# Starting the scans of a hybrid attention–MLP–Mamba kernel from 256 tokens of two batches

## The chip, the cores and the metric

The kernel runs on one core of a Trainium2 chip. The metric is the device time of one execution in microseconds. Before the change the median of three runs is 893.15 us (889.9 to 897.59). Engine names are those of the profile: PE is the matrix engine (PEld its weight loads), DVE the vector engine, ACT the scalar engine, POOL the GpSimd engine, SP the engine that issues most DMAs.

## The reference

The input `x` has 4 batches of 1024 tokens with 128 channels. Four residual blocks follow each other:

```
x = x + attention(layernorm(x))          # 16 heads; window of 32 plus every 64th token
x = x + ffn(layernorm(x))                # [h,-h] @ +-1 weights, relu*2, @ +-1, relu*2, @ +-1
x = x + mamba_block(layernorm(x))        # see below; it has its own layernorm and residual
x = x + ffn(layernorm(x))                # the same weights again

mamba_block(x):                          # per batch, E = 256 inner channels, N = 16 states
  xn = layernorm(x) * ln_g + ln_b
  u, z = split(xn @ W_in)
  u2 = silu(causal_conv(u, 4 taps) + conv_b)
  dt_lo, Bm, Cm = split(u2 @ W_xp);  dt = softplus(dt_lo @ W_dt + b_dt)
  h_t = exp(dt_t * A) * h_(t-1) + (dt_t * u_t) * B_t        # sequential over the 1024 tokens
  y_t = sum over N of h_t * C_t;  y = (y + u2 * D) * silu(z)
  return x + res_scale * (y @ W_out)
```

Only the recurrence over `h` ties the tokens of a batch together in order; two batches are independent of each other.

## The kernel before

**Layout.** `x` stays in SBUF as two tiles, one for each pair of batches (`xs[bp]`). A tile of `xs` holds 64 tokens of each batch of the pair, so a chunk `c` of four such tiles is 512 rows: 256 tokens of both batches. A pair has four chunks.

**Stages.** Attention runs first (to about 246 us). Then chunk by chunk: the first MLP (`mlp`, called by `early`), the norms of the Mamba block (`mamba_norm`: statistics, a power on POOL, scaling on ACT, four transposes on PE, and `mxnT`, the transposed rows that the block reads), its preparation (`mamba_pre_half`: convolution folded into eight matmuls `pc`, silu to `u2`, projection `px`, `pd`, softplus to `dt`, the product `du`), then the scans, the output projection (`mamba_out`, `mamba_out_own`) and the second MLP (`late`, `late_batch`).

**Scans.** The scans are cut into eight parts of 512 tokens of one batch, in the order of line 911: for each pair the first halves of both batches, then the second halves. A part has 16 units, one for each state `n`, each over 256 channels (two halves `h` of 128 partitions). One unit is: two decays `da` on ACT into PSUM, one product `db` on POOL, two scans `hs` on DVE (`tensor_tensor_scan`), and the product `hc` with C, on DVE from `pcc` that PE spreads into PSUM, or for three units in sixteen on POOL. Pairs of `hc` are added by a DMA, and PE sums them into `pys`. In a first half a scan starts from 0.0 and its last column is copied into `carry[b % 2]` (one tile per batch, line 904); in a second half it starts from that column.

**Order of work.** MLP, norm and preparation are written as generators that yield a `Piece` with an estimated cost per engine; a `Work` runs one. Ahead of the scans (lines 1390 to 1413, eight PSUM banks) the loop goes round robin over `mamba_norm` of chunks 0 and 1, the preparation of part 0 and two `lanes` of MLP chunks, holding the lanes back only when the preparation's next piece is for PE. Lane 0 starts with chunk 0, lane 1 with chunk 1, then chunks 2 and 3. Inside the scans (from line 1414, three spare banks) `pieces` is called twice in a unit and issues pieces into the gaps by a model of the engines' times and by allowances per unit (`RATES`: 2.9 us of PE, 1.2 of DVE, 2.4 of ACT, 1.2 of POOL). Emission order is kept as program order there. A unit asks ahead for what it needs: `load_b` three units ahead, `drive` two ahead; if the part that they ask for isn't prepared, `ready` (line 1360) issues pieces without regard to allowances until it is. `hurry` (line 991) lifts the allowance of a preparation's PE pieces eight units before its part begins.

Part 0 needs the preparation of 512 tokens of batch 0, and so chunks 0 and 1 through MLP and norm.

Of the kernel before, what the change touches and what calls it, by code (L numbers as in the profile page):

```python
# [26 lines left out]
P = 128  # L27
# [16 lines left out]
def hybrid_kernel(ctx: ExitStack, tc: tile.TileContext, x, Wq, Wk, Wv, Wo, ln_g, ln_b, W_in, conv_w,  # L44
# [789 lines left out]

    def early(bp, c, *args):
        stats = yield from awaited(("a", bp, c))
        tiles = xs[bp][:, 4 * c : 4 * c + 4, :]
        yield from mlp(f"a{bp}_{c}", tiles, True, *args, hasty=bp == 1 and c < HALF, stats=stats)
        fed.add(("a", bp, c))
# [64 lines left out]
    carry = [mw.tile([P, NH, N], F32, name=f"carry{b2}") for b2 in range(2)]  # L904
# [6 lines left out]
    parts_in_order = [(b, f) for bp in range(NP) for f in range(2) for b in (2 * bp, 2 * bp + 1)]  # L911
# [6 lines left out]
    def mamba_norm(bp, c):  # L918
# [5 lines left out]
        before = order_of[2 * bp, f] - 4  # L924
# [4 lines left out]
        yield Piece(gp=2.7)  # L929

        rs = small.tile([P, 5, 4], F32, tag="rs2", name=f"rs_z{u}", bufs=2)
        gp.tensor_scalar_add(rs[:, 0], mv[:, :, 1], EPS)
        gp.tensor_scalar(rs[:, 1], mv[:, :, 1], 1.0 + EPS, EPS * EPS, ALU.mult, ALU.add)
        both = rs[:, 0:2].rearrange("p a n -> p (a n)")
        gp.tensor_tensor(both, both, minus_half, ALU.pow)
        gp.tensor_scalar_mul(rs[:, 4], mv[:, :, 0], -1.0)
        gp.tensor_mul(rs[:, 2:4], rs[:, 0:2], rs[:, 4:5].to_broadcast([P, 2, 4]))
        gp.tensor_scalar_add(rs[:, 0], rs[:, 0], 1.0)
# [15 lines left out]
        yield Piece(sc=1.6, same=True)  # L954
        ln_apply(tiles, tiles, rs[:, 0], rs[:, 2])
        yield evict(sc=0.6)
# [4 lines left out]
        )  # L961
        fed.add(("n", bp, c))

    def gate_of(v, gate, xnT):
        yield fill(1.8, 2, loose=True)
        pz = [bank(f"pz{v}_{h}") for h in range(NH)]
        for h in range(NH):
            te.matmul(pz[h], w_in[:, E + h * P : E + (h + 1) * P], xnT[:, DC - 1 :], start=True, stop=True)
# [4 lines left out]
    def mamba_pre_half(b, f):  # L973

        bp, b2, place = b // 2, b % 2, order_of[b, f]
        yield Piece(
            ready=lambda: all(("n", bp, c) in fed for c in range(f * HALF, (f + 1) * HALF))
# [4 lines left out]
        xnT = mamba_in[bp, f][:, b2, :]  # L982
        gate = m2.tile([P, NH, CH], F32, name=f"gate{v}", tag="gate", bufs=4)
        if place:
            yield from gate_of(v, gate, xnT)
# [12 lines left out]
        for h in range(NH):  # L998
            for k in range(DC):
# [3 lines left out]
                elif k % 2 == 0:  # L1003
                    yield Piece(pe=1.8, urgent=hurry)
                te.matmul(
                    pc[h], w_conv[:, k, h * P : (h + 1) * P], xnT[:, k : k + CH], start=k == 0, stop=k == DC - 1
                )
        yield evict(lump=True, sc=3.9)
# [18 lines left out]
        if not place:  # L1027
            yield Piece(1, evict=True, ve=1.4)
            ve.tensor_copy(bc, px[: 6 * N])
            ve.tensor_sub(res[: 4 * N], px[: 4 * N], bc[: 4 * N])  # L1030
            yield Piece(-1, urgent=hurry, sc=1.8)
        else:
            yield Piece(1, evict=True, sc=1.8)
            sc.copy(bc, px[: 6 * N])
        sc.copy(dtl[6 * N :], px[6 * N : 6 * N + DR])
        sc.copy(w, px[: 2 * N])
        nc.sync.dma_start(bd, w)
        prepared.add((b, f, "b"))
        if not place:
            sc.copy(bc[: 4 * N], res[: 4 * N])  # L1040
        else:
# [11 lines left out]
        yield evict(lump=True, sc=3.9)  # L1053
        for h in range(NH):
            sc.activation(dt[:, h], pd[h], AF.Softplus, bias=bdt_t[:, h : h + 1])
        if not place:
            ve.tensor_sub(res[: 2 * N], res[: 2 * N], bc[: 2 * N])
        yield urgent(sc=0 if place else 0.6)
        if not place:
            sc.copy(bc[: 2 * N], res[: 2 * N])  # L1060
        for h in range(NH):
            yield urgent(gp=1.3)
            gp.tensor_mul(du[:, h], dt[:, h], u2[:, h])
            prepared.add((b, f, h))
        if not place:
            yield from gate_of(v, gate, xnT)

    def mamba_out(bp, f):

        pair = [(2 * bp + b2, f) for b2 in range(2)]  # L1070
        yield Piece(ready=lambda: all(("g", *k) in fed for k in pair), same=True)
        for q in range(HALF):
            yield fill(2.0)
            po = bank(f"pmo{bp}_{f}{q}")
            for b2 in range(2):
                if b2:
                    yield more(2.0)
                gate = mamba_pre[pair[b2]][0]
                for i in range(4):
                    t0 = (4 * q + i) * R  # L1080
# [399 lines left out]
```

## Time and profile before

| | us |
|---|---|
| median of the runs | 893.15 |
| the profiled execution | 896.53 |
| its span, first to last instruction | 894.7 |
| attention ends, first MLP begins | about 246 |
| first scan starts | 322.93 |
| scans, eight parts of 16 units | 322.9 to 852.2 |
| tail after the scans | 852.2 to 894.7 |

| engine | busy us | share of the span |
|---|---|---|
| PE | 757.9 | 85% |
| DVE | 726.9 | 81% |
| POOL | 682.5 | 76% |
| ACT | 606.3 | 68% |

The shares are averages over attention, a lead-in, the scans and a tail, which have different limits; what matters below is the busy time within a stretch. In the lists, a line of a group gives its engine, operation, tiles, shapes and count, then busy time and the mean of one in ns, then the idle time before it and what ended that. The parts of the scans start at 322.9, 388.5, 457.0, 519.7, 588.6, 655.1, 726.8 and 790.2 us.

### The profile page before, as it was taken

To read this page: it belongs to the slowest core of one execution; us is meant where nothing else is said; L and a number is where in the kernel's file an instruction comes from. 1 tells how busy PE (TensorE), PEld (TensorE's weight loads), DVE (VectorE), ACT (ScalarE), POOL (GpSimd) and SP (SyncE) were. 2 spreads that over 40 slices of the span, in tenths; PEclk is the share of its full clock that TensorE was granted. 3 is DMA by queue.
4 is the path that set the end of the run, shared out by engine and by line. 5 is a ranking of instruction groups with operands and counts; after the bars stand their busy time and mean duration, and the time that the engine had idled before them with its cause. 6 is when DMAs were issued, how large, how long until landed. Compare 5 with 4: busy or idle time off the path is not lost. (4 is left out here: it accounts for less than half of the span.)

```text
span 894.7 us, 16435 instructions
## 1 busy us (share of the span) xinstructions
PE 757.9 (85%) x6204; PEld 465.8 (52%) x6204; DVE 726.9 (81%) x970; ACT 606.3 (68%) x1358; POOL 682.5 (76%) x525
## 2 busy tenths in 40 slices
PE   5798878966788977788989788989889689889898
PEld 2455546645667653334546554535545345656567
DVE  6699998999563258898899998898988779999942
ACT  3776656754364488887878778878967766664523
POOL 6689966999342079999989998979979879877800
PEclk9899989997679989797999999899989799999999
DMA  4743133330010036564564656555565545666410
GB/s 127 129 74 73 27 57 68 74 70 2 3 48 1 1 109 155 127 159 129 137 148 130 153 130 153 145 121 138 155 154 133 141 112 150 164 145 153 108 25 19
DMA packets 59808, 92.77 MB, mean 104 GB/s; under 512 B 6200, under 2 KB 39776, under 8 KB 59728
## 3 DMA queue, kind: packets, MB, share of 16 engines
q1 hardware_dynamic: 49488, 58.15, 22.6%
q0 software_dynamic: 9680, 33.30, 19.8%
q8 instruction: 49, 0.80, 0.4%
q10 hardware_dynamic: 560, 0.26, 0.1%
q14 instruction: 31, 0.25, 0.1%
HBM read 52.11 MB, written 4.72 MB: 64 GB/s over the span
## 5 line engine op out<-in xcount | busy, mean ns | idle before, releaser
L57 POOL TENSOR_TENSOR db<-du,bs 128x1024 f32<-128x1024 f32 x128 | 315.6, 2504 | 23.8 <-DVE hs L57 20.1
L57 ACT ACTIVATE da<-dt,a_t 128x512 f32<-128x512 f32 x256 | 175.2, 687 | 107.1 <-DVE hs L57 106.8
L57 DVE TENSOR_TENSOR_SCAN hs<-da,db 128x512 f32<-128x512 f32 x128 | 149.9, 1209 | 29.7 <-ACT da L57 29.5
L57 DVE TENSOR_TENSOR_SCAN hs<-da,carry,db 128x512 f32<-128x512 f32 x128 | 156.7, 1266 | 5.5 <-ACT da L57 5.2
L57 PE MATMUL pys<-hc,ident 128*128 128x512 f32 x258 | 145.3, 649 | 1.9 <-DMA hc<-hc 1.8
L57 DVE TENSOR_TENSOR hc<-hs,pcc 128x1024 f32<-128x1024 f32 x104 | 126.7, 1218 | 22.1 <-PE pcc L57 15.9
L57 POOL TENSOR_TENSOR prodv<-vS,E 128x128 f32<-128x128 f32 (+14 forms) x30 | 69.6, 2319 | 12.2 <-ACT E L57 11.9
L57 PE MATMUL pga<-h1a,w 128*128 128x512 f32 x256 | 72.4, 435 | 5.1 <-ACT u L57 2.9
L57 PEld LDWEIGHTS pys<-hc,ident 128*128 128x128 f32 x258 | 49.6, 208 | 43.6 <-issue 37.2
L57 POOL TENSOR_TENSOR prod<-kv,qs 128x128 f32<-128x128 f32 (+14 forms) x30 | 71.3, 2376 | 1.0 <-DVE or L57 1.0
L57 POOL TENSOR_TENSOR hc<-hs,cs 128x1024 f32<-128x1024 f32 x24 | 58.1, 2421 | 13.6 <-DVE hs L57 11.6
L57 PE MATMUL pc<-mxnT,w_conv 128*128 128x512 f32 x128 | 63.3, 624 | 4.3 <-DVE h1b L57 2.4
L57 PEld LDWEIGHTS pga<-h1a,w 128*128 128x128 f32 x256 | 51.2, 201 | 27.4 <-issue 4.3
L57 POOL DMA_DIRECT2D hc<-hc x63 | 62.7, 995 | 1.8 <-issue 0.9
L57 ACT ACT_TABLE_LOAD x48 | 61.6, 1283 | 3.5 <-issue 2.6
L57 PE MATMUL pcc<-bc,spread 96*128 96x512 bf16 x104 | 42.0, 404 | 22.5 <-DVE hc L57 21.7
L57 ACT ACTIVATE E<-S 128x512 f32<-128x512 f32 (+15 forms) x62 | 26.5, 472 | 38.8 <-DVE S L57 38.6
L57 PE MATMUL ps<-kx,qT 64*32 64x256 f32 x1008 | 46.2, 432 | 6.3 <-DVE S L57 5.0
L57 POOL TENSOR_TENSOR du<-dt,u 128x512 f32<-128x512 f32 x16 | 24.8, 1551 | 29.7 <-ACT dt L57 29.6
L57 PEld LDWEIGHTS pc<-mxnT,w_conv 128*128 128x128 f32 x128 | 25.2, 199 | 37.4 <-issue 31.9
L57 ACT COPY ep<-pt 128x512 f32<-128x512 f32 x32 | 18.8, 587 | 36.4 <-DVE eo L57 36.1
L57 PE MATMUL pgb<-h1b,w 128*128 128x512 f32 x128 | 38.0, 447 | 1.4 <-ACT u L57 1.4
(245 smaller groups left out, 1682.9 us busy)
## 6 DMA issues: line engine op xcount, KB each, us to landing
bs<-bd SPq DMA_DIRECT2D x64, 512.0 KB
hc<-hc POOLq DMA_DIRECT2D x63, 512.0 KB, 4.6
vr<-vd SPq DMA_DIRECT2D x32, 256.0 KB
cs<-bd SPq DMA_DIRECT2D x24, 256.0 KB
vd<-kv SPq DMA_DIRECT2D x8, 256.0 KB
x<-in_L_attn_a_x_dram SPq DMA_DIRECT2D x15, 128.0 KB
kx<-kT SPq DMA_DIRECT2D x104, 16.0 KB
out_dram<-x SPq DMA_DIRECT2D x8, 128.0 KB
```

The source lines that it names most:

```text
L57: ins = getattr(self.engine, name)(*args, **kwargs)
```

## The change

The first two parts are no longer (batch 0, first half) and (batch 1, first half) but two quarters: 256 tokens of both batches side by side, in tiles of the same width of 512. So part 0 needs chunk 0 alone. A quarter's scan of 512 columns becomes two of 256, one per batch, and the second quarter's scans start from `carry`, which is now one tile. `mamba_out` runs per quarter.

Chunk 0's MLP is halved: each lane takes 256 of its 512 rows (`early_half`). The lanes' chunks are then 1, 3, 5, 7 and 2, 4, 6. Ahead of the scans only the two half chunks run at first; then the chain of norm, transposes and preparation of part 0 is issued in its order, and the lanes' next pieces are let in where the model of the engines' times says that they end before the chain's next piece. Chunks 1 to 3 otherwise run among the scans.

Small edits ahead of the first scan: five operations of the first `rs` move from POOL to DVE (the power stays), `mxnT` is written before the scaling of `x`, the split of B and C into three bf16 rows moves behind `pd` and partly from ACT to POOL, `du` of part 0 and half of the first `db` go to DVE.

```diff
         yield Piece(ready=lambda: key in known, same=True)
         return known[key]
 
+    def early_half(lane, *args):
+        stats = yield from awaited(("a", 0, 0))
+        at = slice(2 * lane, 2 * lane + 2)
+        yield from mlp(f"a0_0{lane}", xs[0][:, at, :], True, *args, stats=stats[:, :, at])
+        fed.add(("half", lane))
+        if all(("half", k) in fed for k in range(2)):
+            fed.add(("a", 0, 0))
+
     def early(bp, c, *args):
         stats = yield from awaited(("a", bp, c))
         tiles = xs[bp][:, 4 * c : 4 * c + 4, :]
-        yield from mlp(f"a{bp}_{c}", tiles, True, *args, hasty=bp == 1 and c < HALF, stats=stats)
+        yield from mlp(f"a{bp}_{c}", tiles, True, *args, hasty=c == 1 or (bp == 1 and c < HALF), stats=stats)
         fed.add(("a", bp, c))
...
-    carry = [mw.tile([P, NH, N], F32, name=f"carry{b2}") for b2 in range(2)]
+    carry = mw.tile([P, NH, 2, N], F32, name="carry")
...
-    parts_in_order = [(b, f) for bp in range(NP) for f in range(2) for b in (2 * bp, 2 * bp + 1)]
+    QUARTER = "quarter"
+    QT = CH // 2
+    parts_in_order = [(QUARTER, 0), (QUARTER, 1)]
+    parts_in_order += [(b, f) for bp in range(NP) for f in range(2) for b in (2 * bp, 2 * bp + 1)][2:]
...
         mv = yield from ln_sums(tiles, f"z{u}", soon=bp == 0)
-        yield Piece(gp=2.7)
+        by = ve if bp + c == 0 else gp
+        yield Piece(gp=2.9 if by is ve else 2.7)
 
         rs = small.tile([P, 5, 4], F32, tag="rs2", name=f"rs_z{u}", bufs=2)
-        gp.tensor_scalar_add(rs[:, 0], mv[:, :, 1], EPS)
-        gp.tensor_scalar(rs[:, 1], mv[:, :, 1], 1.0 + EPS, EPS * EPS, ALU.mult, ALU.add)
+        by.tensor_scalar_add(rs[:, 0], mv[:, :, 1], EPS)
+        by.tensor_scalar(rs[:, 1], mv[:, :, 1], 1.0 + EPS, EPS * EPS, ALU.mult, ALU.add)
...
-        yield Piece(sc=1.6, same=True)
-        ln_apply(tiles, tiles, rs[:, 0], rs[:, 2])
-        yield evict(sc=0.6)
+        yield evict(sc=0.75)
         t0 = DC - 1 + c % HALF * 4 * R
         sc.activation(
             mamba_in[bp, f][:, :, t0 : t0 + 4 * R].rearrange("p b (m r) -> p m b r", r=R),
             tp.rearrange("p (m b r) -> p m b r", b=2, r=R), AF.Identity, bias=b_t, scale=g_t,
         )
+        fed.add(("t", bp, c))
+        yield Piece(sc=1.6, same=True)
+        ln_apply(tiles, tiles, rs[:, 0], rs[:, 2])
         fed.add(("n", bp, c))
 
...
+    def tokens_of(b, f):
+
+        if b == QUARTER:
+            return lambda k: mamba_in[0, 0][:, :, f * QT + k : f * QT + k + QT]
+        return lambda k: mamba_in[b // 2, f][:, b % 2, k : k + CH]
+
+    def like_tokens(b, bk):
+        return bk.rearrange("p (b t) -> p b t", b=2) if b == QUARTER else bk
...
+        place = order_of[b, f]
+        needs = [("t", 0, f)] if b == QUARTER else [("t", b // 2, c) for c in range(f * HALF, (f + 1) * HALF)]
         yield Piece(
-            ready=lambda: all(("n", bp, c) in fed for c in range(f * HALF, (f + 1) * HALF))
+            ready=lambda: all(k in fed for k in needs)
             and (place < 4 or ("o", *parts_in_order[place - 4]) in fed),
...
-                    pc[h], w_conv[:, k, h * P : (h + 1) * P], xnT[:, k : k + CH], start=k == 0, stop=k == DC - 1
-                )
-        yield evict(lump=True, sc=3.9)
+                    like_tokens(b, pc[h]), w_conv[:, k, h * P : (h + 1) * P], xnT(k), start=k == 0, stop=k == DC - 1
+                )
+        yield evict(lump=True, sc=3.9 if place else 1.0)
...
-        if not place:
-            yield Piece(1, evict=True, ve=1.4)
-            ve.tensor_copy(bc, px[: 6 * N])
-            ve.tensor_sub(res[: 4 * N], px[: 4 * N], bc[: 4 * N])
-            yield Piece(-1, urgent=hurry, sc=1.8)
-        else:
+        if place:
             yield Piece(1, evict=True, sc=1.8)
             sc.copy(bc, px[: 6 * N])
+        else:
+            yield Piece(1, evict=True, sc=0.6)
         sc.copy(dtl[6 * N :], px[6 * N : 6 * N + DR])
-        sc.copy(w, px[: 2 * N])
-        nc.sync.dma_start(bd, w)
-        prepared.add((b, f, "b"))
-        if not place:
-            sc.copy(bc[: 4 * N], res[: 4 * N])
-        else:
+        if place:
+            sc.copy(w, px[: 2 * N])
+            nc.sync.dma_start(bd, w)
+            prepared.add((b, f, "b"))
             for rows in (4 * N, 2 * N):
...
-        yield evict(lump=True, sc=3.9)
+        if not place:
+            yield Piece()
+            sc.copy(w, px[: 2 * N])
+            nc.sync.dma_start(bd, w)
+            prepared.add((b, f, "b"))
+            ve.tensor_copy(bc, px[: 6 * N])
+            ve.tensor_sub(res[: 4 * N], px[: 4 * N], bc[: 4 * N])
+            gp.tensor_copy(bc[: 4 * N], res[: 4 * N])
+            ve.tensor_sub(res[: 2 * N], res[: 2 * N], bc[: 2 * N])
+            gp.tensor_copy(bc[: 2 * N], res[: 2 * N])
+        yield evict(lump=True, sc=3.9 if place else 1.9)
         for h in range(NH):
             sc.activation(dt[:, h], pd[h], AF.Softplus, bias=bdt_t[:, h : h + 1])
-        if not place:
-            ve.tensor_sub(res[: 2 * N], res[: 2 * N], bc[: 2 * N])
-        yield urgent(sc=0 if place else 0.6)
-        if not place:
-            sc.copy(bc[: 2 * N], res[: 2 * N])
         for h in range(NH):
-            yield urgent(gp=1.3)
-            gp.tensor_mul(du[:, h], dt[:, h], u2[:, h])
+            yield urgent(gp=1.3) if place else urgent(ve=0.6)
+            (gp if place else ve).tensor_mul(du[:, h], dt[:, h], u2[:, h])
             prepared.add((b, f, h))
         if not place:
-            yield from gate_of(v, gate, xnT)
...
+    def mamba_out(bp, f, *quarters):
+
+        pair = [(QUARTER, q) for q in quarters] or [(2 * bp + b2, f) for b2 in range(2)]
...
-                gp.tensor_tensor(dbs[i], mamba_pre[b, f][3], bs.unsqueeze(1).to_broadcast([P, NH, CH]), ALU.mult)
+                if i:
+                    gp.tensor_tensor(dbs[i], mamba_pre[b, f][3], bs.unsqueeze(1).to_broadcast([P, NH, CH]), ALU.mult)
+                    return
+                for h, by in enumerate((ve, gp)):
+                    by.tensor_mul(dbs[i][:, h], mamba_pre[b, f][3][:, h], bs)
...
-                first = carry[b % 2][:, h, n : n + 1] if f else 0.0
-                ve.tensor_tensor_scan(hs[:, h], das.pop((i, h)), db[:, h], first, ALU.mult, ALU.add)
-                done["hs", i, h] = spend("ve", 1.235 if f else 1.175, *after(("da", i, h), ("db", i)))
+                da = das.pop((i, h))
+                spans = [(b2, slice(b2 * QT, (b2 + 1) * QT)) for b2 in range(2)] if b == QUARTER else [(b, slice(0, CH))]
+                for b2, ts in spans:
+                    first = carry[:, h, b2 % 2, n : n + 1] if f else 0.0
+                    ve.tensor_tensor_scan(hs[:, h, ts], da[:, ts], db[:, h, ts], first, ALU.mult, ALU.add)
+                us = (1.235 if f else 1.175) + 0.07 * (len(spans) - 1)
+                done["hs", i, h] = spend("ve", us, *after(("da", i, h), ("db", i)))
...
-            if f == 0:
-                sc.copy(carry[b % 2][:, :, n : n + 1], hs[:, :, CH - 1 :])
+            if b == QUARTER:
+                sc.copy(carry[:, :, :, n], hs.rearrange("p h (b t) -> p h b t", b=2)[:, :, :, QT - 1])
+            elif f == 0:
+                sc.copy(carry[:, :, b % 2, n : n + 1], hs[:, :, CH - 1 :])
             decay(i + 1, 1)
-            done["da", i + 1, 1] = spend("sc", 0.67 if f else 0.86, *after(("hs", i, 1)))
...
-        return [m2.tile([P, 2, CH], F32R, name=f"h1{u}_{f}", tag="hc", bufs=6) for f in range(4)]
...
+
     lanes = [
         Work(stream(
-            early(0, lane, f1, lane, *[in_scan_buffers] * lane),
-            early(0, 2 + lane, f1, lane),
-            early(1, lane, f1, lane),
-            early(1, 2 + lane, f1, lane),
+            early_half(lane, f1, lane, *[in_scan_buffers] * lane),
+            *(early(bp, c, f1, lane) for bp, c in (((0, 1), (0, 3), (1, 1), (1, 3)), ((0, 2), (1, 0), (1, 2)))[lane]),
...
-        first = [
-            Work(stream(*(mamba_norm(0, c) for c in first_half))),
-            Work(mamba_pre_half(*parts_in_order[0])),
-        ]
+        lead, pre = Work(mamba_norm(0, 0)), Work(mamba_pre_half(*parts_in_order[0]))
         turn = 0
-        while (*parts_in_order[0], NH - 1) not in prepared:
+        while ("a", 0, 0) not in fed:
             turn += 1
             if turn == 12:
...
-            wanted = first[-1].may() and "pe" in first[-1].next.us
-            for w in first + ([] if wanted else lanes):
+            for w in lanes:
                 if w.may():
                     w.run()
-        for w in lanes:
-            while w.next.evict or w.held:
-                w.run()
+        aside = True
+        while (*parts_in_order[0], NH - 1) not in prepared:
+            w = lead if ("t", 0, 0) not in fed else pre
+            if not w.count:
+                w.since = lead.since
+            issue(w)
+            if pre.held and lead.next:
+                issue(lead)
+            if aside and (QUARTER, 0, "b") in prepared:
+                aside = False
+                for v in lanes:
+                    while v.next.evict or v.held:
+                        issue(v)
+            for v in lanes:
+                while aside and v.may() and max(ends(v)[0].values(), default=0.0) < w.since + 0.3:
+                    issue(v)
     with banks(SPARE), tc.tile_pool(name="wide", bufs=1, space=PSUM) as wide:
         keep.append(True)
         works.extend([
-            first[-1],
+            pre,
             Work(stream(*(mamba_pre_half(*k) for k in parts_in_order[1:]))),
-            Work(stream(*(mamba_norm(0, c) for c in second_half), *(mamba_norm(1, c) for c in range(CT)))),
-            Work(stream(mamba_out(0, 0), mamba_out(0, 1), *(mamba_out_own(*k) for k in parts_in_order[4:-1]))),
...
-                        ("b", 0, c), [("o", b, c // HALF) for b in range(2)],
+                        ("b", 0, c), [("o", b, c // HALF) for b in range(2)] if c >= HALF else [("o", QUARTER, c)],
```

## The prediction, made before the result was known

> **What bounds the kernel now.** I first cut the execution into stretches and read each engine's busy time in them (from:to, length, then PE, PEld, DVE, ACT, POOL busy with counts, granted PE clock, DMA share, GB/s).
>
> ```profile
> 250.00:281.70 31.70, 30.32 (x153) 25.17 (x152) 12.53 (x24) 13.19 (x27) 8.40 (x13) 0.87 0.07 13
> 281.70:322.90 41.20, 37.85 (x151) 25.67 (x151) 10.36 (x23) 25.93 (x49) 10.70 (x16) 0.96 0.10 34
> 322.90:852.20 529.30, 458.76 (x1642) 257.21 (x1641) 474.26 (x465) 405.47 (x861) 466.39 (x339) 0.92 0.56 140
> 852.20:894.70 42.50, 36.77 (x268) 31.25 (x266) 12.14 (x34) 12.67 (x37) 1.26 (x2) 0.98 0.05 13
> ```
>
> Ahead of the scans PE is busy nearly all the time and DVE two fifths of it or less; in the scans DVE (90%), POOL (88%) and PE (87%) are all near full and none is full. So an early start of the scans helps only if work that leaves the lead-in fits into 55 us of idle DVE and 70 us of idle PE. The parts of the scans show how tight that is:
>
> ```profile
> 322.90:388.50 65.60, 51.66 (x130) 23.75 (x129) 55.99 (x63) 57.92 (x121) 61.40 (x49) 0.82 0.48 128
> 388.50:457.00 68.50, 57.74 (x172) 29.46 (x171) 59.96 (x60) 55.70 (x126) 61.69 (x44) 0.90 0.59 148
> 457.00:519.70 62.70, 56.89 (x241) 35.70 (x240) 60.47 (x57) 51.30 (x123) 57.48 (x49) 0.95 0.52 132
> 790.20:852.20 62.00, 54.20 (x237) 34.49 (x236) 61.32 (x68) 32.50 (x58) 47.59 (x29) 0.95 0.58 140
> ```
>
> The part at 457.0 has PE 91% and DVE 96% busy and is among the shortest; the last is at 99% of DVE. A full PE doesn't by itself slow a part; DVE is the floor. The first two parts, which the change rebuilds, have 9.6 and 8.5 us of idle DVE and 14 and 11 of idle PE, at a lower clock.
>
> The floor of a unit is two scans and, in 13 of 16, one `hc`, from the list of groups:
>
> ```profile
> L57 DVE TENSOR_TENSOR_SCAN hs<-da,db 128x512 f32<-128x512 f32 x128 | 149.9, 1209 | 29.7 <-ACT da L57 29.5
> L57 DVE TENSOR_TENSOR_SCAN hs<-da,carry,db 128x512 f32<-128x512 f32 x128 | 156.7, 1266 | 5.5 <-ACT da L57 5.2
> ```
>
> Two are issued back to back in 2.34 us, `hc` in 1.22: 16 x 2.34 + 13 x 1.22 = 53 us a part, of 62 to 72.
>
> **Part by part. (A) The lead-in.** Four lines of the timeline (start, duration) mark today's chain:
>
> ```profile
> 280.90 0.75 DVE L57 SCALAR_TENSOR_TENSOR x<-pfoa,total,x 128x512 f32<-128x512 f32 x1
> 300.98 7.03 PE L57 MATMUL pc<-mxnT,w_conv 128*128 128x512 f32 x16
> 316.81 1.27 ACT L57 ACTIVATE dt<-pd,bdt 128x512 f32<-128x512 f32 x2
> 322.93 2.34 DVE L57 TENSOR_TENSOR_SCAN hs<-da,db 128x512 f32<-128x512 f32 x2 [8.35 <-ACT da L57]
> ```
>
> Chunks 0 and 1 end their MLP at 281.65; 41.3 us later the first scan starts. In between PE interleaves chunks 2 and 3 with the chain: `pc` waits for 32 `pfoa` (297.4 to 301.1) though `mxnT` is there at 297.0.
>
> *A1, the MLP.* The tail of this kernel runs exactly two halves of 256 rows:
>
> ```profile
> 877.87 2.13 PE L57 MATMUL pfc<-fxnTc,w 128*128 128x256 f32 x16 [0.33 <-ACT fxnTc L57]
> 879.84 7.73 PE L57 MATMUL pgc<-h1c,w 128*128 128x256 f32 x64
> 887.41 3.73 PE L57 MATMUL pfoc<-w,h2c 128*128 128x128 f32 x32
> ```
>
> From the first `pfc` to the last result (891.66) that is 13.8 us. Today chunks 0 and 1 resume at 254.3, when DVE is through the folding of the convolution weights and gives the low halves of `fxnT`, and end at 281.65. After: 254.3 + 13.8 = 268, a half to one us more for the low clock at 250 to 258. T0 = 269, or 264 if the smaller `fxnT` is split before those weights.
>
> *A2, from T0 to the first scan,* with today's rows and nothing in between: statistics of four tiles 1.6; `rs` 2.4 (the power 1.68 stays on POOL, five small operations of about 0.15); `mxn` 1.65; last transpose 0.35; `mxnT` 0.8; `pc` 7.05; second `u` 0.75; second half of `px` 1.0; `dtl` 0.65; sum 16.25. Then ACT copies `w` 0.58, loads a table 1.28, softplus 1.27, a table 1.28, `da` 0.69: 5.1. Beside that `w` goes through DRAM to `bs`: 1.7 us to the issue of `bs` (313.38 to 315.02), which has landed by 320.2, so 5.2 more at most; with half a `db` on DVE that is up to 8.1 after `dtl`. Together 21.4 to 24.4; I take 23. First scan at 292, bounds 286 to 295.
>
> *A3, the clock.* Today chunks 2 and 3 keep PE busy through this chain and the clock reads 1.00 from 300 to 323. After, PE has little for 6 to 7 us before `pc`: the model's rule lets in, by my count of its pieces, the transposes and `pf` of chunk 1 and the transposes of chunk 2, 4 us. Where PE idled today the clock fell (0.69 in 322.9 to 334, `pz` 1.06 instead of 0.45 us). A cold `pc`, `px`, `pd` costs 0 to 9 us; I take 1. [...]
>
> Lead-in: 322.9 to 293, **-30 us** (-21 to -37).
>
> **(B) Halved scans.** No 256-wide scan is in the trace. The nearest pair is the same DVE operation at both widths:
>
> ```profile
> L57 DVE SCALAR_TENSOR_TENSOR h1c<-pfc,h1c 128x256 fp32r<-128x256 f32 x16 | 5.8, 417 | 3.6 <-ACT h1c L57 3.6
> L57 DVE SCALAR_TENSOR_TENSOR h1c<-pfc,h1c 128x512 fp32r<-128x512 f32 x8 | 5.1, 673 | 0.0
> ```
>
> Two halves cost 2 x 417 - 673 = 161 ns more; issued back to back (0.75 for two of 256, 1.29 for two of 512) 0.105 us more. 32 units x 2 = 64 extra scans: 6.7 to 10.3 us. The second quarter starts from `carry` where today's second part starts from 0: 64 scans x 0.047-0.057 = 3 to 3.6. It lies on the engine that is the floor, so I count it in full: **+11** (0 if it only fills idle DVE, at most 14). [...]
>
> **(C) Work that moves in among the scans.** PE: today all of chunks 2 and 3 but 32 `pfoa` is done ahead. After, by my count, chunk 1 lacks 32 `pg` and 32 `pfo` (11.2), chunks 2 and 3 some 13 and 14: 38 less today's 4, so 34 us of PE for 70 idle. DVE: three `x` and 12 `h1` and `fxnT`, less today's one `x` and what is done ahead, about 6, and chunk 1's statistics 1.8: 8 us for 55 idle. In exchange chunks of the second pair (22 us of PE in the second part: 6.9 `pfa`, 10.7 `pga`, 4.0 `pfoa`) move to later parts. If all of it fits: 0. If it displaces PE one for one: +34. The part at 457.0 (91% and 96%) is nearest to what is asked, and it was short: I take **+4**.
>
> **(D) New due times.** The second part's `b` must be ready at unit 13 and its `du` at unit 14, 57 us after the start at 4.1 us a unit. It needs chunk 1. Rest of its MLP: 11.2 us of PE among scans; the nearest row, chunk 3's last 32 `pfoa`, took until 336.4, 13.5 us after the first scan, so 20 to 25. Norm and preparation took 41 us unhindered in the lead-in, and 48 among scans (326.5 to 374.3). So the scans wait 20 + 41 - 57 = 4 us to 25 + 48 - 57 = 16 us. Pieces issued by `ready` don't ask for allowances, so I take the lower end, **+4**. While they wait, PE and ACT work and DVE, POOL stand.
>
> The rest is small: `mamba_out` has as many matmuls as before; `carry` is copied in 32 units as before (185 ns); DMA counts and bytes, SP's queue included, stay; moving `du` and half a `db` to DVE shortens A2 and is in it.
>
> **The sum:** -30 + 11 + 4 + 4 = **-11** us against this execution's 896.5, so 885.5. This execution is 3.4 us above the median of the runs, so 882 as a median.
>
> **The rivals.**
> 1. *The gain comes back as PE time.* From 250 to 852 PE is idle 75 us in all; if the planner can't use gaps shorter than a piece (2 us), C is +15 and the time 893. For: DVE waited 15.9 us for `pcc` behind such pieces. Against: the part at 457.0.
> 2. *Slower: the scans wait for chunk 1 at unit 13.* At the upper end D is 16; the third part, which needs chunks 2 and 3 (27 us of PE behind chunk 1 and the second preparation, at 2.9 us a unit about unit 20, norms and preparation another 10) waits 5 to 15 as well at unit 29. With C at 8 the sum is -30 + 11 + 8 + 30 = +19: 912. It decides once waits at the two borders exceed about 20 us together.
> 3. *The chain isn't shortened:* ACT, which is strictly in order, takes the lanes' `fxn` (1.65) and casts between the chain's steps, or the clock stays low. Start at 302, sum -2: 891.
>
> **How the numbers follow.** The forecast's own range is 864 to 884 (A at -37 with B at 7 and no waits: -30, down to -9); chance 0.56. Rival 1 0.14, rival 3 0.10, rival 2 0.20 (half of it beyond 907). One per cent, 9 us, is about what a measurement of this kernel can tell from no change: below 884 faster 0.56, to 902 the same 0.23, above 0.21. The range leaves out a tenth on each side: 864 to 907.
>
> **What would show it.** A: first `hs` at 286 to 295, `pc` next on PE after the last transpose, T0 near 269. B: `hs` of 256 columns near 0.69 us, x128. C: PE clock and busy share up in the first four parts, a part at 68 to 72 us. D: gaps on DVE ending in `da` before units 14 to 16 and 30 to 32. Wrong would be a first scan later than 300, or parts 0 and 1 together above 160 us (134 today).

## The result, and the profile after

The changed kernel takes 928.49 us (median, 926.33 to 930.09) beside 891.74 us for the kernel before (889.9 to 897.59). The ratio is 1.040 with a 95% interval of 1.034 to 1.046: **slower by 37 us**, where 882 was forecast and 864 to 907 was the range.

The chain into the first scan, in the timeline of the changed kernel (start and duration in us, engine, operation, tiles, and in brackets the idle time before it with its releaser):

```profile
264.86 0.48 DVE L57 SCALAR_TENSOR_TENSOR x<-pfoa,total,x 128x256 f32<-128x256 f32 x1 [0.57 <-PE pfoa L57]
...
272.21 9.68 PE L57 MATMUL pcquarter<-mxnT,w_conv 128*128 128x512 f32 x16 [1.28 <-ACT mxnT L57]
...
287.06 1.26 ACT L57 ACTIVATE dtquarter<-pdquarter,bdt 128x512 f32<-128x512 f32 x2
...
292.31 2.43 DVE L57 TENSOR_TENSOR_SCAN hs<-da,db 128x256 f32<-128x256 f32 x4
```

The half chunks end at 265.3, `pc` follows at 272.2, and the first scan starts at 292.3 instead of 322.9. The lead-in did what it was meant to do: 30.6 us are won here. The stretches that follow (from:to, length, then PE, PEld, DVE, ACT, POOL busy with counts, granted PE clock, DMA share, GB/s) show where they went:

```profile
250.00:292.30 42.30, 32.49 (x141) 22.10 (x142) 14.29 (x37) 19.49 (x36) 8.47 (x11) 0.78 0.11 34
292.30:1000.00 707.70, 538.76 (x2095) 318.32 (x2094) 501.46 (x581) 432.01 (x927) 472.27 (x348) 0.93 0.42 105
```

The same two stretches of the kernel before, up to its first scan and behind it (a window that ends at 1000 runs past the end of the span):

```profile
250.00:322.90 72.90, 68.17 (x303) 50.84 (x303) 22.89 (x45) 39.12 (x75) 19.10 (x29) 0.92 0.09 25
322.90:1000.00 677.10, 495.53 (x1908) 288.46 (x1906) 486.40 (x498) 418.14 (x898) 467.65 (x341) 0.93 0.44 110
```

Behind the first scan the mean PE clock is 0.93 in both, so it isn't a slower clock there that costs the time. The changed kernel's two quarters, its third part and its tail:

```profile
292.30:371.60 79.30, 65.75 (x218) 37.80 (x218) 58.57 (x91) 54.86 (x119) 60.48 (x43) 0.84 0.41 106
371.60:470.40 98.80, 79.70 (x259) 43.68 (x259) 68.81 (x110) 65.30 (x163) 70.37 (x67) 0.86 0.41 99
470.40:540.00 69.60, 59.12 (x223) 34.19 (x223) 62.32 (x61) 51.86 (x100) 57.38 (x40) 0.95 0.53 132
863.00:928.00 65.00, 53.81 (x359) 45.35 (x358) 15.53 (x45) 18.52 (x49) 2.98 (x6) 0.91 0.04 13
```

The two quarters take 79.3 and 98.8 us where the first two parts took 65.6 and 68.5: 44 us lost. The six other parts, 470.4 to 863.0, take 392.6 us, 2.6 less than before. The tail is 65.0 us instead of 42.5: 22.5 us lost. The balance of the spans is -30.6 + 44.0 - 2.6 + 22.5 = +33.3, which is 928.0 - 894.7.

**What fills the two quarters.** From the first scan to the end of the span PE is busy 538.8 us (before: 495.5) and idle 635.7 - 538.8 = 96.9 us (before: 571.8 - 495.5 = 76.3). PE's work of the whole execution hardly grew (763.7 us busy, before 757.9). It moved. Ahead of the scans, from 250 us on, PE now does 32.49 us at a clock of 0.78, about 25.3 us at full clock (an estimate, busy time times mean clock); before it was 68.17 at 0.92, 62.7. So **37 us of PE work** moved from the lead-in to behind the first scan. DVE's waits in the two quarters (us in total, times, the longest) are mostly one kind:

```profile
DVE hs L57 <- ACT da L57: 38.7, 6, 22.3
DVE hc L57 <- PE pcc L57: 10.2, 4, 6.2
```

The two long ones, 12.2 and 22.3 us, stand before the scans of units 14 and 30 (counted from 0), right behind the units in which the next part's preparation is asked for:

```profile
360.38 2.43 DVE L57 TENSOR_TENSOR_SCAN hs<-da,db 128x256 f32<-128x256 f32 x4 [12.22 <-ACT da L57]
...
456.43 2.67 DVE L57 TENSOR_TENSOR_SCAN hs<-da,carry,db 128x256 f32<-128x256 f32 x4 [22.28 <-ACT da L57]
```

**What fills the tail.** The MLP results that are added last tell it: before, the last two of 512 columns are added from 822.0 and 842.3 us on, both ahead of the end of the scans at 852.2. After, the last but one is added at 852.7, and the last at 880.9, 18 us after the end of the scans at 863.0:

```profile
852.68 0.74 DVE L57 SCALAR_TENSOR_TENSOR ox<-pfoc,total,ox 128x512 f32<-128x512 f32 x1
...
880.93 0.75 DVE L57 SCALAR_TENSOR_TENSOR ox<-pfoc,total,ox 128x512 f32<-128x512 f32 x1 [0.95 <-PE pfoc L57]
```

So more than half of one more MLP lies behind the scans (19 of the 32 matmuls of its middle layer and all 32 of its output), with more of the last output projections (64 matmuls `pmo_1own` where it was 32), and there the other engines have little to do (DVE 15.5 of 65.0 us). This gives three suspects: the halved scans (B of the prediction), the waits at the borders (D), and the 37 us of PE work itself (C).

### The profile page after: what moved, and what is told of

Same layout as the page of the kernel before. It is cut to its first block, busy times and chain, and to the rows that moved or that the text cites. A ratio compares the mean times of both kernels' runs of the same rounds, so it can differ in the third digit from the quotient of the medians.

```text
span 928.0 us, 16618 instructions
## 1 busy us (share of the span) xinstructions
PE 763.7 (82%) x6244; PEld 467.9 (50%) x6244; DVE 736.9 (79%) x1048; ACT 604.0 (65%) x1361; POOL 680.3 (73%) x520
## 5 line engine op out<-in xcount | busy, mean ns | idle before, releaser
L57 POOL TENSOR_TENSOR db<-du,bs 128x1024 f32<-128x1024 f32 x96 | 236.6, 2495 | 23.1 <-DVE hs L57 16.1
L57 DVE TENSOR_TENSOR_SCAN hs<-da,carry,db 128x512 f32<-128x512 f32 (+1 forms) x192 | 199.6, 1087 | 30.0 <-ACT da L57 28.4
L57 ACT ACTIVATE da<-dt,a_t 128x512 f32<-128x512 f32 x192 | 131.4, 687 | 84.2 <-DVE hs L57 83.5
L57 DVE TENSOR_TENSOR_SCAN hs<-da,db 128x256 f32<-128x256 f32 (+1 forms) x128 | 113.7, 938 | 23.8 <-ACT da L57 23.7
L57 PE MATMUL pys<-hc,ident 128*128 128x512 f32 x194 | 103.9, 623 | 2.9 <-DMA hc<-hc 2.9
L57 PE MATMUL pga<-h1a,w 128*128 128x512 f32 (+1 forms) x288 | 81.7, 439 | 12.4 <-DVE h1a L57 5.1
L57 POOL TENSOR_TENSOR db<-duquarter,bs 128x1024 f32<-128x1024 f32 (+1 forms) x32 | 77.9, 2472 | 2.3 <-DMA bs<-bdquarter 1.7
L57 PEld LDWEIGHTS pga<-h1a,w 128*128 128x128 f32 x288 | 57.6, 223 | 40.2 <-ACT h2a L57 6.3
L57 ACT ACTIVATE da<-dtquarter,a_t 128x512 f32<-128x512 f32 x64 | 43.9, 688 | 32.8 <-DVE hs L57 32.7
L57 PE MATMUL pc<-mxnT,w_conv 128*128 128x512 f32 x96 | 45.8, 604 | 0.2 <-ACT gate L57 0.2
L57 PE MATMUL pgc<-h1c,w 128*128 128x256 f32 (+1 forms) x192 | 36.7, 348 | 4.4 <-DVE h1c L57 4.2
```

The costliest lines, as they stand in the source:

```text
L57: ins = getattr(self.engine, name)(*args, **kwargs)
```

## Experiments

**The halved scans alone** (on the kernel before; 512 tokens of one batch a part, as there):

```diff
-                ve.tensor_tensor_scan(hs[:, h], das.pop((i, h)), db[:, h], first, ALU.mult, ALU.add)
+                da = das.pop((i, h))
+                spans = [slice(0, CH // 2), slice(CH // 2, CH)] if b < 2 and not f else [slice(0, CH)]
+                for ts in spans:
+                    ve.tensor_tensor_scan(hs[:, h, ts], da[:, ts], db[:, h, ts], first, ALU.mult, ALU.add)
```

> The kernel before, with each scan of its first two parts cut into two of 256 columns; both start from 0, so the hand-over of the state in the middle of those parts is left out. Theory (the scans wait at two borders for the chain of chunks 1 to 3): the halved scans are nearly free. After shows four of 256 in 2.43 us where before shows two of 512 in 2.34, so 32 x 0.09 = 3 us: 892 + 3, at most + 7. Rival (the halved scans, being on the fullest engine, stretch every unit): the first two parts together grow by 20 us or more, 912 or above.

Measured: 892.3 us beside 892.07, ratio 1.0003 (0.998 to 1.0026). Its groups of scans (busy us, mean ns of one, then idle before):

```profile
L57 DVE TENSOR_TENSOR_SCAN hs<-da,db 128x256 f32<-128x256 f32 x128 | 77.8, 668 | 20.8 <-ACT da L57 18.7 <-POOL db L57 1.8
L57 DVE TENSOR_TENSOR_SCAN hs<-da,db 128x512 f32<-128x512 f32 x64 | 75.0, 1208 | 9.7 <-ACT da L57 9.7
```

The same columns cost 77.8 us of DVE as 128 halves and 75.0 us as 64 wholes: 2.8 us, 44 ns for each extra scan, and none of it can be seen in the time. Halving the scans is no suspect. In the changed kernel the second quarter's start from `carry` comes on top (2.67 instead of 2.43 us a unit, 3.8 us of DVE in 16 units); this run leaves it out, so its part in the time is not shown.

**The waits taken away.** The norms of chunks 1 to 3 no longer wait for their MLP, so the scans' data don't depend on it. The values change, but all the work is still done:

```diff
-            same=True, ready=lambda: ("a", bp, c) in fed and (before < 0 or (*parts_in_order[before + 1], 0) in prepared)
+            same=True, ready=lambda: (("a", bp, c) in fed or (bp == 0 and c > 0)) and (before < 0 or (*parts_in_order[before + 1], 0) in prepared)
```

> The kernel after, but the Mamba norms of chunks 1 to 3 do not wait for the MLP of their chunk (they read x before it, which changes the values; every instruction is still there). Theory (due times): the gaps of DVE before units 14 and 30 go, the first two parts take 66 to 72 us each instead of 79 and 99, so 928 - 41 = 887, plus up to 20 us of MLP that now ends after the last scan: 887 to 907. Rival (the PE work that left the lead-in costs its time wherever it runs): the first two parts stay above 160 us together or the tail takes all of it back, 915 to 928.

Measured: 936.52, ratio to the kernel before 1.0505 (1.0485 to 1.0525), a miss for both theories: 8 us slower than the changed kernel. Stretches of this run: the two quarters, the fourth part and the tail.

```profile
293.30:368.20 74.90, 59.47 (x182) 32.80 (x182) 59.48 (x98) 56.91 (x114) 63.76 (x49) 0.85 0.44 114
368.20:439.90 71.70, 62.67 (x221) 33.07 (x219) 64.49 (x97) 54.73 (x122) 59.02 (x43) 0.93 0.52 129
510.00:598.60 88.60, 74.45 (x252) 40.98 (x251) 63.93 (x64) 61.99 (x138) 66.35 (x58) 0.90 0.44 108
863.40:932.30 68.90, 56.99 (x377) 48.27 (x375) 17.45 (x49) 21.27 (x54) 2.97 (x6) 0.93 0.05 16
```

The quarters fall to 146.6 us from 178.1, so the waits did stand there. But the fourth part, at whose end the second pair's first part comes due, now takes 88.6 us (70.4 in the changed kernel), and the tail 68.9. The work that was put off came due elsewhere. The border waits are where the debt, the MLP work that was put off, is collected, not what it is.

**Chunk 1 finished ahead** of the first scan, on the changed kernel, so that the second quarter's preparation can't be late:

```diff
+        while ("a", 0, 1) not in fed:
+            issue(lanes[0])
     with banks(SPARE), tc.tile_pool(name="wide", bufs=1, space=PSUM) as wide:
```

> The kernel after, with the rest of chunk 1's MLP issued ahead of the first scan (some 11 us of PE). Theory (due times): the first scan comes 5 to 10 us later, at 297 to 302, and the wait at unit 13 falls from about 15 us to under 5; chunks 2 and 3 get the PE time that chunk 1 used, and the wait at unit 29 falls from about 27 to 10-20: 905 to 918. Rival (PE time): nothing but the place of the work changes, 924 to 932.

Measured: 936.98 (1.0501, 1.0485 to 1.0516). The first scan starts at 303.4, the first quarter takes 67.3 us and its border wait is gone; the second takes 94.2, with 21.9 us in one unit at its end, and the tail 68.8. Another miss: one border mended, the whole worse.

**The chain ahead of the lanes, without quarters** (on the kernel before, lanes held once chunks 0 and 1 are through):

```diff
-            for w in first + ([] if wanted else lanes):
+            chunks_done = all(("a", 0, c) in fed for c in first_half)
+            for w in first + ([] if wanted or chunks_done else lanes):
```

> The kernel before, with one part of the change alone: once chunks 0 and 1 are through their MLP the lanes are held back until the first part is prepared, so the chain has PE to itself and chunks 2 and 3 run among the scans; parts and scans are as before. Theory (due times): the first scan comes at 306 to 310 instead of 323; nothing waits at unit 13, since chunk 1 is done; chunks 2 and 3 are due at unit 29 and 0 to 10 us of wait stay there: 878 to 890. Rival (PE time): the 15 us come back in the parts or in the tail, 890 to 895.

Measured: 913.99 (1.025, 1.0227 to 1.0272), missing both expectations. The first scan starts 9.2 us earlier, at 313.7, and the second part pays more than all of it:

```profile
250.00:313.70 63.70, 48.84 (x182) 30.79 (x180) 14.75 (x35) 26.57 (x48) 17.73 (x27) 0.82 0.08 24
377.80:468.10 90.30, 74.41 (x244) 42.03 (x242) 63.11 (x77) 60.37 (x140) 67.11 (x61) 0.89 0.43 105
```

There is no quarter and no halved chunk in this kernel, yet its second part looks like the changed kernel's second quarter: 90.3 us, PE 74.4 of them. What they share is MLP work of the first pair that is no longer done ahead.

**Quarters without holding the lanes back** (the changed kernel, but chunks 0 and 1 are whole, one per lane, and the lead-in is the kernel before's loop, which issues the lanes round robin):

```diff
-            early_half(lane, f1, lane, *[in_scan_buffers] * lane),
-            *(early(bp, c, f1, lane) for bp, c in (((0, 1), (0, 3), (1, 1), (1, 3)), ((0, 2), (1, 0), (1, 2)))[lane]),
+            early(0, lane, f1, lane, *[in_scan_buffers] * lane),
+            early(0, 2 + lane, f1, lane),
+            early(1, lane, f1, lane),
+            early(1, 2 + lane, f1, lane),
...
+            wanted = pre.may() and "pe" in pre.next.us
+            for w in first + ([] if wanted else lanes):
+                if w.may():
+                    w.run()
```

> The quarters without the rest: parts, carry and halved scans as after, but chunks 0 and 1 whole, one on each lane, and the lanes free ahead of the scans as in the kernel before, so PE stays full of chunks 1 to 3 until the first scan. Theory 1: the first scan comes at 305 to 315 and about as much PE work is done by then as PE could do; no wait at unit 13, little at 29: 884 to 896. Theory of the due times alone: chunk 1 is ready, but chunks 2 and 3 still wait at unit 29 by 10 us or more: 895 to 910.

Measured: 912.52 (1.0257, 1.0229 to 1.0285), above both expectations. First scan at 307.5, quarters of 65.2 and 67.2 us, as good as before; then the fourth part (68.9 us in the kernel before) and the tail, in its stretches:

```profile
508.00:588.00 80.00, 65.09 (x183) 33.22 (x183) 58.36 (x54) 62.15 (x141) 66.65 (x60) 0.83 0.46 115
845.90:910.00 64.10, 53.18 (x340) 43.94 (x339) 14.23 (x44) 18.34 (x50) 2.96 (x6) 0.92 0.04 13
```

Neither half of the change gains by itself, and again the loss lies where MLP work comes due. This run and the one ahead of it have the kernel before's chunks on the lanes, so the loss doesn't hang on the changed kernel's uneven lanes.

**More PE work among the scans, nothing else changed** (on the kernel before; the four chunks of the second pair run the matmuls of their middle layer twice, 128 more):

```diff
+                if u.startswith("a1"):
+                    yield more(2.05)
+                    for i in range(4):
+                        w = wt(w1[:, i, (f0 + f) * P : (f0 + f + 1) * P])
+                        for s in range(parts):
+                            te.matmul(pg[f], w, h1[i][:, s], start=i + s == 0, stop=i == 3 and s == parts - 1)
```

> The kernel before, in which the four MLP chunks of the second pair do the 32 matmuls of their middle layer twice (the second time over the first, same result): 128 matmuls of 0.236 us, 30 us more PE work among the scans, and nothing else. It measures the price of a microsecond of PE there. Theory 1 (PE time among the scans costs about one for one): 892 + 25 to 35. My prediction's step C (it goes into 70 us of idle PE): 892 + 0 to 8.

Measured: 940.98 beside 888.79 (1.0575, 1.0528 to 1.0622): 30 us of matmuls at full clock cost 52 us, 1.7 us for each, more than either theory allowed. The stretches are the fourth part (68.9 us in the kernel before), the sixth (71.7) and the tail (42.5):

```profile
517.00:594.70 77.70, 63.90 (x210) 34.43 (x209) 58.86 (x55) 54.88 (x113) 63.95 (x50) 0.93 0.51 125
664.60:749.30 84.70, 71.64 (x259) 40.70 (x259) 59.70 (x60) 56.16 (x129) 64.40 (x49) 0.92 0.49 120
879.10:943.60 64.50, 55.26 (x372) 46.26 (x370) 15.70 (x46) 18.43 (x50) 2.96 (x6) 0.97 0.06 17
```

The same picture without any of the change's edits: parts of 78 and 85 us ahead of a due time, and a tail of 64.5 us with 372 matmuls where it was 268. And PE's idle time from the first scan to the end went up, from 76.3 to 85.6 us (620.9 - 535.3). The gaps took in nothing. The allowances per unit were left as they are, so the price is one at that pace; how much of it is PE's time alone this run doesn't say.

**The same MLP work taken out of either kernel:** chunks 2 and 3 of the first pair are left without their first MLP, some 27 us of PE.

```diff
+        if bp == 0 and c >= HALF:
+            fed.add(("a", bp, c))
+            return
```

> The kernel after without the MLP of chunks 2 and 3 (27 us of PE at full clock; their tokens go on without it). Theory (PE work among the scans is what is short, and the lead-in is where the kernel before does it): the wait at unit 29 goes, the tail comes down from 64 to 42-50, and the time falls by more than the 27 us of PE, 1.2 to 1.7 us for each: 882 to 896. Rival (due times alone): only the wait at unit 29 goes, 27 us at most: 901 to 910.

> The kernel before without the MLP of chunks 2 and 3, the partner of the run above. That work lies mostly ahead of the scans here. Theory: the chain has PE to itself, the first scan comes at 305 to 310, the parts keep their lengths: 870 to 878, a fall of 0.5 to 0.7 us for each us of PE, less than half of what the same work costs in the kernel after. If the work were as dear ahead of the scans as among them, it would be 845 to 860.

Measured together: 900.94 (1.0086, 1.0056 to 1.0117) from the changed kernel and 884.4 (0.9903, 0.9868 to 0.9939) from the one before, whose own time was 891.73. Both are misses for the theory: the first lies at the lower end of its rival, the second above both of its ranges. Against 928.49 and 891.73, leaving out this work is worth **27.5 us in the changed kernel and 7.3 us in the kernel before**. That is the price of the place: ahead of the first scan, beside a chain that leaves PE waiting, the work cost about a quarter of its length; among the scans it costs its whole length. This pair alone can't tell the work from the wait that goes with it; the run without the waits can, since there the wait went and nothing was gained. The second quarter of the changed kernel falls from 98.8 to 67.2 us when it is left out:

```profile
294.40:370.90 76.50, 60.99 (x162) 30.09 (x162) 59.99 (x100) 55.94 (x117) 63.00 (x49) 0.78 0.43 110
370.90:438.10 67.20, 56.08 (x185) 28.46 (x184) 61.78 (x91) 56.65 (x132) 62.13 (x51) 0.91 0.56 139
```

Its tail stays at 62.2 us, against what I expected. The kernel before wins its 7.3 us in the lead-in: its first scan starts 8.1 us earlier, at 314.8, with 21.4 us less PE work ahead of it (62.7 and 41.3, by the reckoning below). The two kernels without this work still differ by 16.5 us, with 15.8 us of other PE work moved (25.5 and 41.3 us ahead of the scans).

**Repairs.** If the debt is the cause, more lane work let in during the chain must help. The bound on what may run aside goes from 0.3 to 2.5 us past the chain's next piece:

```diff
-                while aside and v.may() and max(ends(v)[0].values(), default=0.0) < w.since + 0.3:
+                while aside and v.may() and max(ends(v)[0].values(), default=0.0) < w.since + 2.5:
```

> The kernel after, but ahead of the scans the lanes' pieces are let in if they end within 2.5 us after the chain's next piece, not 0.3. Theory: PE is fuller and its clock higher there (32.5 of 42.3 us busy at 0.78 now), the first scan comes 2 to 6 us later, chunk 1 ends 10 us earlier, and 5 to 15 us are won: 913 to 923. Rival (chain first is right and PE time is not the point): the later start is lost, 930 to 934.

Measured: 909.57 (1.0204, 1.0182 to 1.0226), 19 us better than the changed kernel, more than expected.

```profile
250.00:300.40 50.40, 42.77 (x225) 32.32 (x225) 20.58 (x44) 28.20 (x59) 11.83 (x15) 0.94 0.11 31
300.40:368.50 68.10, 56.39 (x186) 31.95 (x186) 59.64 (x99) 55.19 (x110) 61.55 (x49) 0.91 0.46 121
368.50:448.00 79.50, 62.46 (x191) 32.85 (x191) 64.78 (x97) 54.94 (x121) 60.80 (x44) 0.87 0.50 122
853.40:908.80 55.40, 43.99 (x305) 37.04 (x303) 14.14 (x44) 16.82 (x46) 2.97 (x6) 0.91 0.05 15
```

The first scan starts 8 us later than in the changed kernel, and the end comes 19 us earlier. At 448.0, after two parts, this kernel is 9 us ahead of the one before (457.0); at the end of the scans, 853.4, the lead is gone, and the tail is 12.9 us longer.

The other repair raises the allowances, `RATES`, by half, so that the debt is worked off earlier; once on the changed kernel, once on the one before as a control, once with the wider bound:

```diff
-    RATES = {"pe": 2.9, "ve": 1.2, "sc": 2.4, "gp": 1.2}
+    RATES = {"pe": 4.4, "ve": 1.8, "sc": 3.6, "gp": 1.8}
```

> The kernel after with all four allowances of the planner half as large again (PE 4.4 us a unit instead of 2.9). Theory 1 (the scans can't hold more PE work: a part of 63 us takes 57 us of it, and what left the lead-in costs its time somewhere): units get longer where pieces are let in, the waits at units 13 and 29 get shorter by as much, 920 to 935. Theory 2 (the allowances alone keep the pieces out): the first two parts fall from 178 to 150 or less and the tail from 64 to 45, 885 to 905.

> The kernel before with the same larger allowances, the control of the run above. Theory 1: nothing is late in it, so 888 to 900. Theory 2: PE's idle time in the scans (70 us) shrinks and the tail with it, 875 to 888.

> Both: the lanes let in within 2.5 us and the larger allowances (PE 4.4 us a unit). With the larger allowances alone the kernel after was at 907. Theory: 893 to 903, still not below the kernel before, since the 37 us of PE work at full clock that left the lead-in are only partly back. If the waits were all, 880 to 888.

Measured: 906.95 (1.0209, 1.0171 to 1.0247), 903.86 (1.0162, 1.0134 to 1.019) and 910.31 (1.0213, 1.017 to 1.0255); the first lies between its two theories, the others above theirs. Beside the kernel before as measured with it (888.79) the changed kernel is now 18.2 us slower instead of 36.8, so it gains some 19 us; the kernel before loses 15, and the two repairs together give no more than one. So the pace of 2.9 us a unit suits the kernel before and is too slow for the changed one's debt. No version that does all the work beat the kernel before.

The first two of these runs are a pair of their own: the change, with the larger allowances on both sides. Ahead of the first scan (the changed kernel, then the one before):

```profile
250.00:294.10 44.10, 32.54 (x143) 22.00 (x143) 16.33 (x39) 21.41 (x42) 10.58 (x14) 0.77 0.12 34
250.00:319.90 69.90, 65.17 (x297) 48.65 (x297) 20.32 (x44) 36.54 (x69) 16.46 (x25) 0.94 0.08 22
```

In this pair the change costs 906.95 - 903.86 = 3.1 us, not 37, though as much PE work has moved (61.3 - 25.1 = 36.2 us at full clock). The first scan comes 25.8 us earlier, and from there to the end it takes 610.9 instead of 582.8 us, 28.1 more: 0.8 us for each moved one. So a large part of the 37 us hangs on the planner's pace. The moved work isn't free at the faster pace either, and both kernels are then slower than the kernel before at its own pace.

**All of it in one table.** PE work ahead of the first scan from 250 us on is its busy time there times the mean clock (an estimate, since the mean is over the stretch). Gain and loss are against the kernel before, from the spans of the profiled runs.

| kernel | PE work ahead | moved | first scan, gain | first scan to end | loss | loss per us moved |
|---|---|---|---|---|---|---|
| before | 62.7 | - | 322.9 | 571.8 | - | - |
| changed | 25.3 | 37.4 | 292.3, 30.6 | 635.7 | 63.9 | 1.7 |
| chain first, no quarters | 40.0 | 22.7 | 313.7, 9.2 | 597.8 | 26.0 | 1.1 |
| chunk 1 ahead | 37.6 | 25.1 | 303.4, 19.5 | 631.3 | 59.5 | 2.4 |
| changed, without the waits | 26.7 | 36.0 | 293.3, 29.6 | 639.0 | 67.2 | 1.9 |
| quarters, lanes free | 49.8 | 12.9 | 307.5, 15.4 | 602.5 | 30.7 | 2.4 |
| wider bound | 40.2 | 22.5 | 300.4, 22.5 | 608.4 | 36.6 | 1.6 |
| changed, larger allowances | 25.1 | 37.6 | 294.1, 28.8 | 610.9 | 39.1 | 1.0 |
| before, larger allowances | 61.3 | 1.4 | 319.9, 3.0 | 582.8 | 11.0 | - |
| both repairs | 39.0 | 23.7 | 300.9, 22.0 | 605.7 | 33.9 | 1.4 |

In every row the loss exceeds the gain, and beside the kernel before at its own pace no row pays less than 1 us for a moved one. The faster pace alone costs 11.0 us with almost nothing moved; it is a part of the loss in the two other rows that have it. The kernel with halved scans alone moves almost nothing (62.0 ahead) and loses nothing.

**What stays open.** That moved PE work is not taken in by the gaps is shown; its price is not settled. It is 0.8 us for each where both kernels have the larger allowances, and 1.0 to 2.4 beside the kernel before at its own pace. How much of it is PE's time and how much the pace, no run separates: the doubled matmuls were not run with larger allowances. The tail was 42.5 us with 268 matmuls in it, 55.4 with 305, and 64.1 to 68.9 with 340 to 377. Of the twelve expectations only that for the halved scans was met, so the direction is understood better than the size. Nearly all MLPs share one buffer for the middle layer (`h1`), so a late chunk can hold up the next; a version with a buffer for each lane wasn't tried.

## Why the prediction was wrong

**A, the lead-in, was right** in its steps: -30 predicted, -30.6 measured, first scan at 292.31 (292 to 293 predicted). That it came so close is in part luck. The end of the half chunks was put at 269 and came at 265.3, 3.7 us early, the lower bound's case; the chain behind it took 27.0 us instead of 24 (23, and 1 for the clock, A3). Most of that is the clock: `pc` took 9.68 us instead of 7.03, 2.65 us more, with a granted clock of 0.50 from 272.2 to 277.4 and 1.00 behind that. A3's 1 us, taken out of a range of 0 to 9, was the author's estimate, and no run shows it; what the changed kernel shows is these 2.65 us on `pc`, while `px` (1.88 us for four) and `pd` (1.98) took as long as before. Rival 3, a chain that isn't shortened, is out. The order of ACT that it goes by can be seen once in the kernel before: ACT sat idle for 1.26 us until the `h2a` at 320.24, and a table load, for which the timeline lists no tile to wait for, came only behind it, at 320.86.

**B, +11, was over-sized**; halved scans alone are 0 as a term of the time (1.0003). What failed is the price from a neighbouring operation, 105 to 161 ns per extra instruction, where 44 was measured, and counting it in full "on the engine that is the floor". DVE is the floor of a part only while nothing else is late, and it idles 9.6 and 8.5 us in the kernel before's first two parts. For the start from `carry`, 3 to 3.6 us were predicted and 3.8 us of DVE time measured; what it is worth in the time no run shows.

**C, +4, is the step that failed** and that decided the result. Its count was right: "34 us of PE" were to move, and 37 did. Wrong was "for 70 idle": I took PE's idle time, summed over the scans, for room, and the part at 457.0 (PE 91% busy) for proof that such room can be used. When 30 us were added with nothing else changed, 52 came out and PE's idle time rose; when 37 moved, it rose by 20.6. The part behind the one at 457.0 needs the same chunks, so no chunk comes due at its end; that this is why it was short fits the runs, but none isolates it. The least price that any pair shows, 28.1 us for 36.2 moved, is seven times the +4; the upper end that I gave, "one for one: +34", lies between that and the 63.9 us that B, C and D came to together. Rival 1 named the mechanism, at a price of +15, which is too low. The planner's pace comes into the prediction only as a time in rival 2 (2.9 us a unit); that the price of moved work hangs on it I left out.

**D, +4, had the right places and the wrong nature.** The waits stand behind units 13 and 29, where rival 2 had them, and rival 2's sign came true. The four long units (13, 14, 29 and 30) take 14.6, 7.6, 24.9 and 10.0 us, 57.1, where four units at 4.1 are 16.4: 41 us instead of 4, and 30 at the upper end. But I priced each wait as a chain of latencies from a start to a due time. Without these waits the time went up, not down: they are C's bill, presented at the first due time. With another due time it comes there (the fourth part), and what is left comes in the tail, which the prediction left at 42.5 us without a word. It is 65.0, and 22.5 of the 63.9 us lost behind the first scan lie there.

So the sum was -30 + 11 + 4 + 4 and came out as -30.6 and, for B, C and D together, +63.9. Halving scans explains none of it. At the least prices measured (0.8 to 1.0 us for each) the 37 us of moved PE work explain 30 to 37; how the rest divides between the pace, the due times and the tail is open. The stated sign of failure, "parts 0 and 1 together above 160 us", is there: 178.1.

## What to carry to other kernels

Before work is moved off a chain to shorten it, ask what that chain gave the work for free: MLP chunks beside a latency-bound lead-in cost about a quarter of their PE time (7.3 us for some 27); the same chunks among scans that keep DVE, POOL and PE each near 90% busy (in the kernel before) cost all of it (27.5 us in the changed kernel). Idle time summed over a stage was not room here: 30 us of matmuls put beside 76.3 us of idle PE cost 52. To know the price of displaced work, add a known amount of the same work to the stage and time it. A wait that appears at a due time may be only where a debt is collected: if taking it away moves the loss to the next due time or the tail, reduce the debt, not the wait. And where a planner paces the work, compare before and after at more than one pace: here the same change cost 37 us at one and 3 at another.

## What was unexpected of the hardware

A scan of 256 columns takes 668 ns and one of 512 takes 1209; by these durations two halves are 127 ns dearer, but back to back the records overlap and four halves take 2.43 us where two wholes take 2.34, 45 ns for each extra instruction.

In the lead-in with less beside the chain the granted PE clock is 0.78 (0.92 before), and 32.5 us of busy time there do only about 25 us of full-speed work (an estimate, busy time times mean clock). Part of what this thinner lead-in wins is thus given back to the clock: 2.65 us in `pc`.
